# A gated low-rank FFN behind a per-sample matrix: the block products taken of x itself, the per-sample matrix applied to their rows

## Chip, cores and metric

One Trainium2 chip, one NeuronCore of it. The metric is device time in microseconds, here the median of three runs. All data is fp32.

## What is computed

x is 64 samples of 64 rows and 1024 columns. Each sample picks one of 16 matrices W (64x64), which turns the 64 rows of the sample into 64 tokens. A token is a vector of 1024; there are 4096 tokens.

```
W = weights[condition]
y = einsum('bct,bcd->bdt', x, W)            # 4096 tokens of 1024
scores = y @ Wr.T                           # 64 experts
top_vals, top_idx = top_k(scores, 16)
G = zeros.at[rows, top_idx].set(softmax(top_vals))
h = einsum('nd,krd->nkr', y, A)             # 64 experts x rank 16 = 1024
out = einsum('nkr,kdr->nd', h * G[:, :, None], B)
result = x + 2.0 * out
```

So there are two products with 1024x1024 matrices, "h" (with A) and "o" (with B), a gate between them, a small product with W ahead, and the routing.

## The kernel before

Tokens are worked on in 8 groups of 512 (4 tiles of 128). For each group, in this order:

- `condition` (L165 to L179): 4 tiles of x, each multiplied by its two W's in 64x64 matmuls (four at once, one per quadrant of the array) into PSUM tiles `yp`. ScalarE copies these into `y`, which holds y transposed. W's are fetched by an indirect DMA on GpSimd (`gather`, L129), with indices that VectorE computes from `cond`.
- `scores_t`, `scores` (L187 to L207): y times Wr in 128x256 matmuls (`st`), turned by a small matmul (`sp`); `route`/`route_top` on VectorE find the top 16, with exponentials on ScalarE; `gates` (L305) turns the gates into `gg`.
- the product h = A y, as a Strassen-Winograd scheme: y and A are split into 2x2 blocks of 512x512 (256 tokens), and 7 block products p1 to p7 replace 8. Sums of y's blocks are made on VectorE (`y_sums`).
- the results are added up in `hb` and multiplied by `gg` (L679, or L429 in the first two groups).
- the product o = hb B in the same scheme, added to x (loaded again, tiles `o`), and stored.

**One level and two levels.** Group 0 does both products on one level, group 1 does h on one level: `experts_in` (L398), `experts_out` (L460), which run `seven` (L353), in matmuls of 256 columns (h) or 512 (o). All else is on two levels: each of the 7 block products (a "parent", L569) is itself split into 7 leaf products. `run` (L622) issues one parent: leaf products p1, p2, then p3 of the parent before, p6, p4 of the parent before, then what is hooked in at "mid", then `prepare` of the next parent, then p7, p5, then what is hooked in at "end". `prepare` makes four sums t1 to t4 of the token operand on VectorE (256 elements a partition each); p5, p6, p7, p3 read them. Partial results meet in PSUM banks x, y, w and are combined by three copies and an add chain on ScalarE and VectorE. `done` adds parents up.

In an h parent of before A's leaf is the stationary operand and the tokens move, in matmuls of 128 columns, 4 per leaf product. In an o parent the tokens are stationary and B's leaf moves, 256 columns, 2 per leaf product.

**Leaves.** The 49 leaves of B and 49 of A are made once (VectorE differences, `leaf_steps`, L508) and stored to DRAM. All of B's, and three of each seven of A's, are then fetched for each parent on SP's queue into a ring of 11 buffers, in the order of their use (`order_of_use`, L545; `fetch`, L552, which runs after each use of a leaf). Four leaves of each block of A stay in SBUF. B's leaves are made during group 0's o product through a pool of three buffers (`bsum`), A's during group 1's h product, after the first fetches and residual loads of group 1 are already on the queue.

The order of work is written by hand; each engine runs its instructions in program order, SP too. A DMA on SP's queue also waits for the one that used its completion semaphore before, so some eight are in flight.

Of the kernel before, what the change touches and what calls it, by code (L numbers as in the profile page):

```python
# [15 lines left out]
P = 128  # L16
# [4 lines left out]
TPG = 4  # L21


@with_exitstack
def kernel(
    ctx: ExitStack,
    tc: tile.TileContext,
    x: bass.AP,
    cond: bass.AP,
# [5 lines left out]
):  # L35

# [17 lines left out]
    CH = HT // P  # L54
    HN = TPG * P // 2
    assert 2 * C == P and C == D and KR == T and HT == BANK and TOPK == 16
# [5 lines left out]
    xp = ctx.enter_context(tc.tile_pool(name="xp", bufs=4))  # L62
    small = ctx.enter_context(tc.tile_pool(name="small", bufs=2))
    acc = ctx.enter_context(tc.tile_pool(name="acc", bufs=7, space=PSUM))
# [3 lines left out]
    one_level = ctx.enter_context(ExitStack())  # L68
    tmp = one_level.enter_context(tc.tile_pool(name="tmp", bufs=1, side="right"))
    first_group = ctx.enter_context(ExitStack())  # L70
    bpool = first_group.enter_context(tc.tile_pool(name="bpool", bufs=1, side="right"))
    op = first_group.enter_context(tc.tile_pool(name="op", bufs=5, side="right"))
# [9 lines left out]
    cond_b = const.tile([P, B], I32)  # L82
    nc.sync.dma_start(cond_b, cond.to_broadcast([P, B]))
    xs = {}

    def load_x(i: int):
        xs[i] = xp.tile([P, T], F32, tag="x", name=f"x_{i}")
        nc.sync.dma_start(xs[i], x[ts(i, P), :])

    def load_block(name, src, r, c, pool=apool):  # L90
        t = pool.tile([P, CH, BANK], F32, name=name)
        nc.sync.dma_start(t, src[ts(r, HT), ts(c, BANK)].rearrange("(c p) k -> p c k", p=P))
        return t

    load_x(0)
    load_x(1)
    a11 = load_block("a11", a_t, 0, 0)
    load_x(2)  # L100
    load_x(3)
# [36 lines left out]
    wr_sb = const.tile([P, 2 * CH, K], F32)  # L138
    nc.sync.dma_start(wr_sb, wr_t.rearrange("(c p) k -> p c k", p=P))

    behind = const.tile([1, 1], F32)
    nc.sync.dma_start(behind, ws[0][0:1, 0, 0:1])
    a21 = load_block("a21", a_t, 0, 1)
    a22 = load_block("a22", a_t, 1, 1)
    a12 = load_block("a12", a_t, 1, 0)
    b12 = load_block("b12", b_t, 0, 1, bpool)
    b22 = load_block("b22", b_t, 1, 1, bpool)
    b11 = load_block("b11", b_t, 0, 0, bpool)
    b21 = load_block("b21", b_t, 1, 0, bpool)

    y, hb, yt = {}, {}, []
    for i in range(2):
        yt.append(blocks.tile([P, 2 * CH, HN], F32, name=f"y{i}"))
        for j in range(2):
            y[j, i] = yt[i][:, ts(j, CH), :]
            hb[i, j] = blocks.tile([P, CH, HN], F32, name=f"hb{i}{j}")
    gg = blocks.tile([P, TPG * P], F32, name="gg")

    def condition(g: int, i: int):

        xt = xs.pop(g * TPG + i)  # L165
        yp = [acc.tile([P, 2 * CH, D], F32, tag="acc", name=f"yp_{g}_{i}_{j}") for j in range(2)]
        for c in range(2 * CH):
            for j in range(2):
                r = slice(j * C, (j + 1) * C)
                for e in range(2):  # L170
                    nc.tensor.matmul(  # L171
                        yp[j][e * D : (e + 1) * D, c, :],
                        lhsT=xt[r, ds(c * P + e * D, D)],
                        rhs=ws[g][r, i, :],
                        start=True,
                        stop=True,
                    )
        for j in range(2):
            nc.scalar.copy(yt[i // 2][:, :, ds(i % 2 * P + j * D, D)], yp[j])  # L179

    def scores_t(g: int):

        st = ps_s.tile([P, 2, HN], F32, tag="s", name=f"st_{g}")
        for h in range(2):
            for c in range(2 * CH):
                e = slice((c % 2) * K, (c % 2 + 1) * K)
                nc.tensor.matmul(  # L187
                    st[e, h, :],
                    lhsT=wr_sb[:, c, :],
                    rhs=y[c // CH, h][:, c % CH, :],  # L190
                    start=(h == 0 and c < 2),
                    stop=(c >= 2 * CH - 2),
                    skip_group_check=True,
                )
        st_sb = small.tile([P, 2 * HN], F32, tag="st_sb", name=f"st_sb_{g}", bufs=1)
        nc.scalar.copy(st_sb, st.rearrange("p h n -> p (h n)"))
        return st_sb

    def scores(g: int, st_sb):

        sp = ps_s.tile([P, TPG, K], F32, tag="s", name=f"sp_{g}")
        for i in range(TPG):
            nc.tensor.matmul(
                sp[:, i, :], lhsT=st_sb[:, ts(i, P)], rhs=two_i, start=True, stop=True
            )
        scs = small.tile([P, TPG, K], F32, tag="sc", name=f"sc_{g}", bufs=1)
        nc.vector.tensor_copy(scs, sp)  # L207
        return scs

    def route(g: int, scs, i: int):  # L210

        sc = scs[:, i, :]
        top = small.tile([P, 16], F32, tag="top", name=f"top_{g}_{i}")
        left = small.tile([P, K], F32, tag="left", name=f"left_{g}_{i}", bufs=1)
        left2 = small.tile([P, K], F32, tag="left2", name=f"left2_{g}_{i}", bufs=1)
        nc.vector.max(top[:, 0:8], sc)
        neg = small.tile([P, 1], F32, tag="neg", name=f"neg_{g}_{i}")
        nc.vector.tensor_scalar(neg, top[:, 0:1], -1.0, None, ALU.mult)
        e = small.tile([P, K], F32, tag="e", name=f"e_{g}_{i}")
        nc.scalar.activation(e, sc, AF.Exp, bias=neg, scale=1.0)  # L220
        nc.vector.match_replace(
            out=left, in_to_replace=top[:, 0:8], in_values=sc, imm_value=TAKEN
        )
        nc.vector.max(top[:, 8:16], left)
        nc.vector.match_replace(
            out=left2, in_to_replace=top[:, 8:16], in_values=left, imm_value=TAKEN
        )
        gu = small.tile([P, K], F32, tag="gu", name=f"gu_{g}_{i}", bufs=1)
        total = small.tile([P, 1], F32, tag="total", name=f"total_{g}_{i}")
        nc.vector.scalar_tensor_tensor(  # L230
            gu, left2, TAKEN, e, ALU.is_le, ALU.mult, accum_out=total
        )
        inv = small.tile([P, 1], F32, tag="inv", name=f"inv_{g}_{i}")
        nc.vector.reciprocal(inv, total)
        g2 = small.tile([P, 2, K], F32, tag=f"g2_{i}", name=f"g2_{g}_{i}", bufs=1)
        nc.vector.tensor_scalar(
            g2,
            gu.unsqueeze(1).to_broadcast([P, 2, K]),
            inv,
            SCALING,  # L240
            ALU.mult,
            ALU.mult,
        )
        return g2

    def route_top(g: int, scs):

        top = rt.tile([P, TPG, 16], F32, tag="tops", name=f"tops_{g}")
        neg = rt.tile([P, TPG], F32, tag="negs", name=f"negs_{g}")
        e = rt.tile([P, TPG, K], F32, tag="es", name=f"es_{g}")  # L250
        total = rt.tile([P, TPG], F32, tag="totals", name=f"totals_{g}")
        inv = rt.tile([P, TPG], F32, tag="invs", name=f"invs_{g}")
        for i in range(TPG):
            nc.vector.max(top[:, i, 0:8], scs[:, i, :])
        nc.vector.tensor_scalar(neg, top[:, :, 0], -1.0, None, ALU.mult)

        def exps(*tiles):
            for i in tiles:
                nc.scalar.activation(
                    e[:, i, :], scs[:, i, :], AF.Exp, bias=neg[:, i : i + 1], scale=1.0  # L260
                )

        def rest(i):
# [3 lines left out]
                out=left, in_to_replace=top[:, i, 0:8], in_values=scs[:, i, :], imm_value=TAKEN  # L267
# [18 lines left out]
        def scaled():  # L286
            g2s = []
            for i in range(TPG):
                g2 = small.tile([P, 2, K], F32, tag=f"g2_{i}", name=f"g2_{g}_{i}", bufs=1)
                nc.scalar.activation(  # L290
                    g2,
                    e[:, i, :].unsqueeze(1).to_broadcast([P, 2, K]),
                    AF.Copy,
                    scale=inv[:, i : i + 1],
                )
                g2s.append(g2)
            return g2s

        return exps, rest, scaled

    def gates(g: int, g2s):

        gp = ps_s.tile([P, TPG, P], F32, tag="s", name=f"gp_{g}")
        for i in range(TPG):
            nc.tensor.transpose(gp[:, i, :], g2s[i].rearrange("p a k -> p (a k)"), ident)  # L305
        nc.scalar.copy(gg.rearrange("p (i n) -> p i n", n=P), gp)

    t3_pool = [extra]

    def y_sums():  # L310

        operands = {"p1": y[0, 0], "p2": y[1, 0], "p3": y[1, 1], "p5": y[0, 1]}

        def step1():
# [14 lines left out]

        return operands, step1, step2, step3  # L330

    def h_sums():

# [721 lines left out]
```

## Time and profile before

| | us |
|---|---|
| median of 3 runs | 815.12 (814.99 to 816.27) |
| the profiled execution | 819.59 |
| its span, first to last instruction | 817.3 |
| VectorE busy | 611.0 |
| TensorE weight loads busy (beside the matmuls) | 692.1 |
| granted TensorE clock, mean | 0.997 |

The page of a profile lists busy time by engine: PE are matmuls, PEld weight loads, DVE VectorE, ACT ScalarE, POOL GpSimd, SP the queue on which most DMAs are issued. Stretches give busy time in a window of the span; the chain of waits gives what the last instruction hung on; timelines give instructions by start. A program's fp32 matmul shows as two instructions. Lengths of matmuls overlap, so that costs are read from the distance between starts. Most of the data moved is leaves, in lines of the page's sixth part:

```profile
lo_p_p<-o_p_p SPq DMA_DIRECT2D x343, 256.0 KB
lh_p_p<-h_p_p SPq DMA_DIRECT2D x126, 256.0 KB
```

202.48 MB are moved in all, 248 GB/s over the span.

### The profile page before, as it was taken

To read this page: it belongs to the slowest core of one execution; us is meant where nothing else is said; L and a number is where in the kernel's file an instruction comes from. 1 tells how busy PE (TensorE), PEld (TensorE's weight loads), DVE (VectorE), ACT (ScalarE), POOL (GpSimd) and SP (SyncE) were. 2 spreads that over 40 slices of the span, in tenths; PEclk is the share of its full clock that TensorE was granted. 3 is DMA by queue.
4 is the path that set the end of the run, shared out by engine and by line. 5 is a ranking of instruction groups with operands and counts; after the bars stand their busy time and mean duration, and the time that the engine had idled before them with its cause. 6 is when DMAs were issued, how large, how long until landed. Compare 5 with 4: busy or idle time off the path is not lost.

```text
span 817.3 us, 17350 instructions
## 1 busy us (share of the span) xinstructions
PE 792.3 (97%) x6684; PEld 692.1 (85%) x6684; DVE 611.0 (75%) x1275; ACT 198.6 (24%) x507; POOL 35.3 (4%) x39
## 2 busy tenths in 40 slices
PE   2999998999999999999999999999999999999996
PEld 2888544888899988999889998899889998899985
DVE  0768447678897778968698686986879777896886
ACT  1110200102222232222323232332322323222221
POOL 4200200000200010000200002000000000000000
PEclk9999999999999999999999999999999999999999
DMA  8901568865889667894688856797678956787695
GB/s 286 386 32 40 187 232 295 315 234 189 270 268 391 196 208 232 300 386 146 193 285 324 307 168 216 262 364 245 192 221 287 387 181 201 243 304 253 181 301 200
DMA packets 108961, 202.48 MB, mean 248 GB/s; under 512 B 12114, under 2 KB 17490, under 8 KB 108882
## 3 DMA queue, kind: packets, MB, share of 16 engines
q1 hardware_dynamic: 107858, 200.35, 72.6%
q0 software_dynamic: 1024, 1.05, 0.5%
q8 instruction: 53, 0.87, 0.4%
q14 instruction: 26, 0.21, 0.1%
HBM read 166.23 MB, written 35.13 MB: 246 GB/s over the span
## 4 chain that ended last, share of the span: by engine, by line
PE 93%; DVE 2%; DMA 2%; issue 0%; ACT 0%; SPq 0%; DVEq 0%; ACTq 0%
PE o_p_x L596 21%; PE h_p_x L596 18%; PE o_p_w L596 11%; PE h_p_w L596 9%; PE o_p_y L596 5%; PE yp L171 5%; PE h_p_y L596 5%; PE st L187 4%; PE h_x L406 3%; PE h_z L406 3%; PE h_w L406 3%; PE o_z L465 2%; PE o_w L465 1%; PE o_x L465 1%; PE h_y L406 1%; DMA o_p_p<-os_p_p 1%
## 5 line engine op out<-in xcount | busy, mean ns | idle before, releaser
L596 PE MATMUL o_p_x<-lo_p_p,l_t 128*128 128x256 f32 x588 | 144.2, 379 | 0.5 <-ACT l_b L634 0.5
L596 PEld LDWEIGHTS o_p_x<-lo_p_p,l_t 128*128 128x128 f32 x588 | 110.7, 190 | 15.4 <-ACT l_b L634 0.9
L76 DVE TENSOR_TENSOR o<-o,m_o_p 128x1024 f32<-128x1024 f32 x56 | 68.2, 1219 | 0.8
L179 ACT COPY y<-yp 128x512 f32<-128x512 f32 x64 | 34.3, 590 | 90.5 <-PE yp L171 90.5
L171 PEld LDWEIGHTS yp<-w_st,x 64*64 64x64 f32 x2048 | 35.1, 140 | 24.3 <-DMA w_st<-in_cw_dram,idx 12.1
L76 DVE TENSOR_TENSOR m_h_p<-h_p_w,l_a 128x256 f32<-128x256 f32 x42 | 17.8, 423 | 50.5 <-PE h_p_w L596 50.5
L129 POOL DMA_INDIRECT w_st<-in_cw_dram,idx x32 | 34.5, 1078 | 463.7 <-PE yp L171 451.5
L171 PE MATMUL yp<-w_st,x 64*64 64x64 f32 x2048 | 39.8, 227 | 13.9 <-DMA w_st<-in_cw_dram,idx 12.1
L596 PE MATMUL o_p_w<-lo_p_p,l_t 128*128 128x256 f32 x196 | 52.5, 390 | 0.0
L596 PE MATMUL h_p_x<-l_t,lh_p_p 128*128 128x128 f32 x336 | 44.4, 275 | 0.0
L596 PE MATMUL h_p_w<-l_t,lh_p_p 128*128 128x128 f32 x336 | 44.4, 275 | 0.0
L596 PEld LDWEIGHTS h_p_x<-l_t,lh_p_p 128*128 128x128 f32 x336 | 41.4, 192 | 0.3
L596 PEld LDWEIGHTS h_p_w<-l_t,lh_p_p 128*128 128x128 f32 x336 | 41.3, 192 | 0.3
L596 PEld LDWEIGHTS o_p_w<-lo_p_p,l_t 128*128 128x128 f32 x196 | 35.2, 190 | 6.9 <-issue 2.3
L634 ACT COPY l_b<-o_p_x 128x256 f32<-128x256 f32 x49 | 18.3, 373 | 90.7 <-PE o_p_x L596 90.7
L76 DVE TENSOR_TENSOR m_o_p<-o_p_w,l_a 128x256 f32<-128x256 f32 x49 | 20.5, 419 | 24.8 <-PE o_p_w L596 18.3
L76 DVE TENSOR_TENSOR m_o_p<-o_p_w,l_b 128x256 f32<-128x256 f32 x49 | 20.6, 421 | 24.6 <-ACT l_b L634 24.6
L634 ACT COPY l_b<-h_p_x 128x256 f32<-128x256 f32 x42 | 15.6, 373 | 90.8 <-PE h_p_x L596 90.8
L641 ACT COPY m_o_p<-o_p_x 128x256 f32<-128x256 f32 x49 | 18.3, 373 | 64.2 <-PE o_p_x L596 64.2
L406 PE MATMUL h_x<-y,a 128*128 128x256 f32 x128 | 30.4, 394 | 1.1 <-ACT y L179 1.1
L679 DVE TENSOR_TENSOR hb<-hb,gg 128x1024 f32<-128x1024 f32 x24 | 29.4, 1225 | 0.8
L406 PEld LDWEIGHTS h_x<-y,a 128*128 128x128 f32 x128 | 25.1, 198 | 5.6 <-ACT y L179 1.2
(163 smaller groups left out, 1596.5 us busy)
## 6 DMA issues: line engine op xcount, KB each, us to landing
lo_p_p<-o_p_p SPq DMA_DIRECT2D x343, 256.0 KB
lh_p_p<-h_p_p SPq DMA_DIRECT2D x126, 256.0 KB
x<-in_x_dram SPq DMA_DIRECT2D x32, 512.0 KB
o<-in_x_dram SPq DMA_DIRECT2D x28, 512.0 KB
out_dram<-o SPq DMA_DIRECT2D x28, 512.0 KB
o_p_p<-os_p_p SPq DMA_DIRECT2D x28, 256.0 KB
h_p_p<-hs_p_p SPq DMA_DIRECT2D x21, 256.0 KB
a<-in_a_t_dram SPq DMA_DIRECT2D x4, 1024.0 KB
```

The costliest lines, as they stand in the source:

```text
L76: nc.vector.tensor_tensor(o, a, b, ALU.add)
L129: nc.gpsimd.indirect_dma_start(out=w_st[:, i, :], out_offset=None, in_=cw, in_offset=bass.IndirectOffsetOnAxis(ap=idx[:, n : n + 1], axis=0),)
L171: nc.tensor.matmul(yp[j][e * D : (e + 1) * D, c, :], lhsT=xt[r, ds(c * P + e * D, D)], rhs=ws[g][r, i, :], start=True, stop=True,)
L179: nc.scalar.copy(yt[i // 2][:, :, ds(i % 2 * P + j * D, D)], yp[j])
L187: nc.tensor.matmul(st[e, h, :], lhsT=wr_sb[:, c, :], rhs=y[c // CH, h][:, c % CH, :], start=(h == 0 and c < 2), stop=(c >= 2 * CH - 2), sk ...
L406: nc.tensor.matmul(bank[:, ts(s, HN)], lhsT=left[p][:, c, ts(2 * q + s, P)], rhs=right[p][:, c, :], start=first and s == 0 and c == 0, sto ...
L465: nc.tensor.matmul(bank, lhsT=left[p][:, c, ts(m, P)], rhs=right[p][:, c, :], start=first and c == 0, stop=c == CH - 1, skip_group_check=True,
L596: nc.tensor.matmul(bank if kind == "o" else bank[:, ts(s, P)], lhsT=v[:, c, :] if kind == "o" else w[:, c, ts(s, P)], rhs=w[:, c, :] if ki ...
L634: nc.scalar.copy(par["val"][n], par["bank"]["x"])
L641: nc.scalar.copy(pr["q"][0][1], pr["shaped"](pr["bank"]["x"]))
L679: nc.vector.tensor_tensor(hb[i, j], hb[i, j], gg[:, ts(j, HN)].unsqueeze(1).to_broadcast([P, CH, HN]), ALU.mult,)
```

## The change

- The host also hands over x transposed and cut in blocks (`x_t`). The h product is taken of x's rows, not of the tokens: Z = A x per row, in the same scheme with the rows as the stationary operand and A's blocks moving. `gated` then multiplies Z's rows by W, again in 64x64 matmuls (`zp`), and the gate multiplication by `gg` reads these from PSUM and writes `hb`. `condition` and its ScalarE copies go.
- Scores are taken of x's rows too: `scores_t` and `turn` as before, and then `scores`, 8 more 64x64 matmuls with W (`sw`). ScalarE copies both results.
- There is one chain of parents, each on one or two levels. h and o parents have the same form: 256-column leaf products of two matmuls, or, on one level, two halves of four 512-column matmuls each, copied by ScalarE. Group 0 is on one level, and the first four h parents of group 1; the last three are on two levels.
- The sums of A and B are chosen such that both schemes have the form of o. p1, p2, p3 and p5 of A's leaves stay in SBUF. Of three B blocks (p1, p2, p3) the three raw leaves are fetched from B itself and not stored.
- The ring has 14 buffers. In group 1 the first 14 fetches and the residual loads come between A's leaves, in the order p7, p5, p3, fetches, residual loads, p1, p2, p4, p6.
- x_t of the next group is loaded at the end of the first o parent; x was loaded at the first h parent. The scores of the next group are still taken in the o parents; routing of tiles 2 and 3 falls in the first h parent.
- The first load is x_t's block 00 and A's block 11, each in two halves that alternate, and `cond` is loaded on ScalarE's queue.

The core of the diff:

```diff
+    def scores(st):
...
+        for i in range(TPG):
+            for j in range(2):
+                r = slice(j * C, (j + 1) * C)
+                nc.tensor.matmul(
+                    sw[r, i, :], lhsT=ws[g][r, i, :], rhs=st["zr"][r, i, :], start=True, stop=True
+                )
...
+    def gated(st, i, j):
...
+        for c in range(CH):
+            for s in range(2):
+                for b in range(2):
+                    r = slice(b * C, (b + 1) * C)
+                    for e in range(2):
+                        nc.tensor.matmul(
+                            zp[b][e * D : (e + 1) * D, c, s, :],
+                            lhsT=z[r, s, ds(c * P + e * D, D)],
+                            rhs=ws[g][r, 2 * i + s, :],
...
+        for b in range(2):
+            nc.vector.tensor_tensor(
+                tokens(hb[j, i])[:, :, :, b, :], zp[b], g_ij[:, :, :, b, :], ALU.mult
+            )
...
+            for c in range(2):
+                nc.tensor.matmul(
+                    bank,
+                    lhsT=v[:, c, :],
+                    rhs=w[:, c, :],
...
+    load_x(0, 0, 0, 2, (load_a11(0), load_a11(1)))
+    load_x(0, 1, 0)
+    a21 = load_block("a21", a_t, 1, 0, apool)
...
+        lv = {0: (1,) * 7, 1: (1, 1, 1, 1, 2, 2, 2)}.get(st["g"], (2,) * 7)
...
+        if g:
+            at(h + 0, "mid", sums, st, "x_sums", "s3")
...
+            at(h + 0, "mid", rest, st, 2, 3)
...
+        at(h + 2, "mid", load_res, st)
+        if g == 1:
...
+            at(h + 0, "mid", a_leaf, "p7")
+            at(h + 0, "end", a_leaf, "p5")
+            at(h + 1, "mid", a_leaf, "p3")
+            at(h + 1, "end", first_fetches)
+            at(h + 2, "mid", a_leaf, "p1")
+            at(h + 3, "mid", a_leaf, "p2")
+            at(h + 4, "end", a_leaf, "p4")
+            at(h + 5, "end", a_leaf, "p6")
+        if nxt:
...
+            for i, j in ((0, 0), (1, 0), (0, 1), (1, 1)):
+                at(o, "end", load_x, g + 1, i, j)
...
+            at(o + 2, "mid", scores_t, nxt)
```

Here `h + n` and `o + n` are the n-th parent of a group's h and o product, "mid" and "end" the places in `run`.

## The prediction

> **What bounds the kernel now.** I read the page first, then busy time by stretches, then the start of the chain of waits, then the timeline around places where TensorE slows down. The page's first part says which engine counts:
>
> ```profile
> span 817.3 us, 17350 instructions
> PE 792.3 (97%) x6684; PEld 692.1 (85%) x6684; DVE 611.0 (75%) x1275; ACT 198.6 (24%) x507; POOL 35.3 (4%) x39
> ```
>
> TensorE is busy 97%. Busy time by stretches (span of the stretch, then PE, PEld, DVE, ACT, POOL busy with counts, granted clock, DMA share, GB/s):
>
> ```profile
> 402.30:498.60 96.30, 96.30 (x890) 88.33 (x890) 75.94 (x164) 28.36 (x74) 4.28 (x4) 1.00 0.78 259
> 150.00:155.00 5.00, 5.00 (x26) 4.38 (x26) 3.55 (x16) 0.35 (x1) 0.00 (x0) 1.00 1.01 376
> 155.00:160.00 5.00, 5.00 (x26) 4.41 (x25) 2.46 (x4) 0.59 (x1) 0.00 (x0) 1.00 1.05 393
> ```
>
> One steady group of 512 tokens takes 96.3 us and TensorE never rests in it; VectorE has 20 us spare. The other two lines are a burst of loads: the DMA engines give about 385 GB/s when asked. The chain in its first 26 us (start, us, what) and TensorE's timeline (start, us, line, operation):
>
> ```profile
> 0.74 4.43 DMA cond_b<-in_cond_dram
> 6.07 5.94 DMA w_st<-in_cw_dram,idx
> ...
> 20.16 5.16 PE h_x L406 x16
> 25.31 2.02 PE yp L171 x128
> ```
>
> ```profile
> 25.24 2.10 PE L171 MATMUL yp<-w_st,x 64*64 64x64 f32 x128
> 128.67 5.40 PE L465 MATMUL o_z<-b,s 128*128 128x512 f32 x8 [2.16 <-DVE o_b L76]
> 133.90 3.60 PE L465 MATMUL o_w<-bt,hb 128*128 128x512 f32 x8
> 312.14 1.03 PE L596 MATMUL o_p_y<-lo_p_p,s 128*128 128x256 f32 x4
> 313.00 1.89 PE L596 MATMUL o_p_x<-lo_p_p,l_t 128*128 128x256 f32 x8
> 343.43 1.06 PE L596 MATMUL h_p_y<-y,a 128*128 128x128 f32 x8
> 344.32 1.06 PE L596 MATMUL h_p_x<-y,lh_p_p 128*128 128x128 f32 x8
> ```
>
> Lengths overlap, so I cost by distance of starts: a leaf product (two matmuls of 256 columns, or four of 128; each is two instructions) takes 313.00 - 312.14 = 0.86 us in the out product (0.863 over a run of them) and 344.32 - 343.43 = 0.89 (0.893) in the first product. A block product on one level takes 3.43 us per half in 512-column matmuls, 3.454 in 256-column ones.
>
> **The start.** Before, TensorE waits 12.05 us for cond, index and gather; at 25.24 it has done only 2.02 + 3.45 = 5.5 us of full-speed work, so it behaves as if started at 19.8. After, the first product reads x_00 and a11, loaded in halves: 0.25 + 0.5 MB. By stretches the DMAs before had moved 0.83 MB by 6 us; with an estimated 1 us to land, TensorE starts at 7.0. It starts at the low clock: the 5.16 row against 3.45 says 1.7, I take 2. Effective start 9.0: **10.8 saved**. Bounds: data at 6 (11.8) and at 10 (7.8). The later blocks (3 MB by 12 us, 6.3 MB by 20) come before their products, since each product takes 6.9 us. Gathering is now needed only for the scores, past 30 us.
>
> **Stalls of the first group.** At 46.67 a product of 3.45 ends at 50.1 and the next starts at 50.99, after a sum of A: 0.9. At 126.3 the product before the 128.67 row is through: 2.3 idle, plus 5.40 - 3.43 = 2.0 of low clock, because VectorE waited for leaf stores. **5.2 saved**: in the new order the one-level products need only ScalarE's copies of 0.6 us.
>
> **First product.** Groups 2 to 7 go from 49 leaf products at 0.893 to 49 at 0.863: 1.47 each, 8.8. Group 1 had 14 halves at 3.454 = 48.4 and gets 8 at 3.43 plus 21 leaves at 0.863 = 45.6: 2.8. Group 0: 0.3. **11.9 saved.** Here a rule would give less. The Trainium skill (TensorE: Matmul & The Clock Gate, Back-to-back issue gap) gives an isolated warm gap of N/2.4 + 2.5 ns. Taken twice per fp32 instruction it is 111.7 ns for 128 columns, which is the row (0.893/8), but 218.3 for 256, where the row is 215.8. By the rule a group saves 1.0, not 1.47, and the sum loses 2.9. The rows decide.
>
> **W's products move, they don't go.** 128 products of 64x64 per group stay (four runs of about 1.09, same shapes): 0. Two PSUM evictions per run go from ScalarE (0.59 each) into VectorE's gate, which now reads PSUM: 8 of 128x512 at 0.69 (the nearest row, a gate of a PSUM tile in the first groups) = 5.5 for 4 gates of 1.22 = 4.9. VectorE stays at about 76 of 96 us; on average it is cover enough. New are 8 matmuls of W on the scores' rows. No row shows two quadrants at work; four give 0.016 us per instruction, none would give 0.056: 16 instructions are 0.25 to 0.9. I take 0.5 and 0.1 for the switch: **4.8 lost** in 8 groups (2.8 to 8).
>
> **The end.** Before, VectorE does two adds of 1.24 just ahead of the last one. After, one: **1.1 saved**. The last store is the same.
>
> **Waits in a steady group.** VectorE's queue has tight places. At the first parent of a group it now does, ahead of the operands of the third, one x sum (1.2), two tiles' routing (1.05 each by the timeline) and reciprocals (0.4), where before it did one tile. Those operands are first needed 1.73 + 2.59 = 4.3 us after that place. Writing out the queue with 0.34 per 256-element operation (0.46 if dependent) and 1.15 per 1024 (1.25), from the scores on, operand t2 of the second parent comes 0.8 late. The gates are the other place: VectorE waits there for W's products, behind it queue the next parent's operands, and for those TensorE waits; three come in a row, and I find 0.5 to 1 to spare. So 0.8 in each of groups 2 to 7: **4.8 lost** (0 to 12). Next in line behind such a wait is only TensorE itself.
>
> **The jam in group 1.** This is the biggest unknown. VectorE makes A's leaves in group 1's first product, 4 operations of 0.69 for each of seven blocks, while it still makes B's last leaves. Time from the fifth out parent of group 0: VectorE is through with B's leaves at 22.4 without waiting for stores, about 26.5 with (three buffers, as at 126 us before). Then come x sum, routing, leaves of p7, p5, p3, ending near 41. After those SP gets 14 fetches (0.26 MB), then the 4 residual loads (0.52 MB), and only then the stores of the next leaves (p1). A's leaves have three buffers: the leaves of p2 can't be written before p1's stores land. At 385 GB/s the 6.0 MB take 15.7 us, with 2 us of latency (estimate): 58.7. Behind that wait VectorE has 2.8 of leaves and 0.9 until t2 of the first two-level parent: 62.4. TensorE wants t2 at 52.0. That is 10.4 of idling. And the clock: the skill's same page (The HAM clock gate) says it falls after an idle window of about 3.4 us; the 128.67 row lost 2.0 after 2.3 us of idling. By either rule this gap pays, so 2.0 more; VectorE's work in the next parents (6.5 to 7.7 against 6.05) costs another 1. **13.4 lost** (0 if VectorE is some 10 us earlier, 24 if stores go as slowly as at 116 to 130).
>
> **Other moves.** x_t is loaded at the first out parent (2 MB, contiguous) instead of in the next first product; it has 11.4 us until the scores and needs 2/0.385 + 2 = 7. It is moved onto the stretch with the most fetches (1.8 MB per 6 us, 297 GB/s); the ring of 14 holds two parents, 12 us, more than the 5 us that it delays them. 0, up to 6 lost. Three B blocks are fetched raw in 1 KB rows, 9 of 49 fetches: 0, up to 2 lost. Copying scores to ScalarE (24% busy): 0.
>
> **Sum.** Saved 10.8 + 5.2 + 11.9 + 1.1 = 29.0; lost 4.8 + 4.8 + 13.4 = 23.0; net 6.0. The profiled execution took 819.59 (span 817.3, 2.3 around it), so its successor takes 813.6; the median is 4.5 below the profiled one: 815.12 - 6.0 = **809.1**.
>
> **Rivals.** *The cover holds* (0.18): no jam, no late t2. For it: VectorE has 20 us spare per group, and the leaf stage before shows no idle TensorE. Against: there the fetches were issued ahead of all of A's leaves, here between them. 809.1 - 18.2 = 790.9.
> *The jam decides, slower* (0.22): one mechanism, SP's queue with stores behind fetches. At 113 to 131 ten leaf steps took 18 us, 1.8 each; if the last 13 B steps go so, 23.4 in place of 9 plus the 4 of waiting that I allowed, everything behind is 10.5 later: 819.6. It turns the sign once group 1 waits over 13.4 + 6.0 = 19.4 us. Against: fewer raw blocks are stored, and no loads lie among those stores.
> *It doesn't shorten a group* (0.12): the late operand costs 1.8 instead of 0.8 in six groups, so that a steady group stays longer than 96.3, and the gain at the start is eaten: 815.1, no change.
> My forecast has 0.48. The likeliest cases of both signs lie apart; the forecast's own range is 803 to 815.
>
> **Numbers.** Within 0.2% (1.6 us) is about what a measurement can't tell from no change. Faster: 0.46 of the forecast, 0.18, and 0.02 of the third rival; same: 0.02 and 0.10; slower: 0.22. The range 790 to 821 reaches to the first rival's time and a little beyond the slower one's, and leaves out about half of the first and a third of the slower one.
>
> **What would show it.** Start: TensorE's first matmul at 6 to 8 us. First product: 0.863 between starts of leaf products. Steady group: 95.5 to 97 between two score products, with a gap of about 0.8 at the second parent's third operand, released by VectorE. Jam: a gap of some 10 us ahead of group 1's first two-level parent, VectorE waiting for a store of A's p1. No such gap, and I am wrong towards 791; gaps in several places of group 1, and towards 820. A first matmul after 10 us or steady groups over 98 would break the sum too.

## The result, and the profile after

| | before | after |
|---|---|---|
| median, first comparison | 815.48 (814.99 to 816.27, 4 runs) | 822.97 (822.09 to 824.54, 4 runs) |
| median, second comparison, in a later set of runs | 820.16 (818.4 to 821.7, 17 runs) | 823.75 (821.64 to 824.27, 5 runs) |
| the profiled execution, and its span | 819.59, 817.3 | 823.33, 821.3 |
| mean granted TensorE clock | 0.997 | 0.991 |

The change made the kernel slower: the ratio is 1.0093 [1.0075, 1.0111] in the first comparison and 1.0045 [1.0031, 1.0058] in the second. So the loss is under 1% and clear of the noise in both. The changed kernel takes nearly the same time in both. It is the kernel before that varies: four runs at 815 to 816, and all 66 of the later sets at 818.4 to 823.3. The profiled execution of before (819.59) belongs to the second level, and so does a second profile of it that was taken later (821.08); steady groups are 96.36 long in both.

The page's first lines after:

```profile
span 821.3 us, 14798 instructions
PE 788.6 (96%) x5448; PEld 617.6 (75%) x5448; DVE 614.0 (75%) x1279; ACT 194.4 (24%) x509; POOL 32.8 (4%) x39
```

TensorE is busy for 3.7 us less and rests for longer: 25.0 us idle before, 32.7 after. So the question is where it rests. Its timeline after, at the start and in group 1 (start, us, line, operation, and in brackets the idle time just before and who ended it):

```profile
8.49 16.61 PE L459 MATMUL h_p<-a,x 128*128 128x512 f32 x32 [8.49 <-DMA a<-in_a_t_dram]
25.04 3.67 PE L180 MATMUL st<-x,wr_sb 128*64 128x256 f32 x32
...
150.67 1.16 PE L303 MATMUL zp<-w_st,m_h_p 64*64 64x64 f32 x64 [2.08 <-DVE m_h_p L81]
...
156.16 1.03 PE L493 MATMUL h_p_y<-at,x 128*128 128x256 f32 x4
169.08 2.05 PE L493 MATMUL h_p_x<-lh_p_p,l_t 128*128 128x256 f32 x4 [11.90 <-issue]
...
174.29 1.03 PE L493 MATMUL h_p_x<-a,sum_p 128*128 128x256 f32 x4
```

From 25.04 to 148.6 TensorE never rests: group 0's stalls are gone. Ahead of 150.67 it waits 2.1 us for a sum on VectorE. At 156.16 + 0.86 it wants operand t2 of the first two-level parent and gets it at 169.08, 12.1 us late. The next three leaf products then take 5.2 us (169.08 to 174.29) where 2.6 is normal. Who holds the operand is seen on VectorE's timeline, and why on SP's (columns as above; on SP the length is that of issuing):

```profile
165.31 0.69 DVE L84 TENSOR_TENSOR hs_p_p<-a 128x512 f32<-128x512 f32 x1 [12.09 <-DMA h_p_p<-hs_p_p]
```

```profile
145.89 3.79 SPq L425 DMA_DIRECT2D lh_p_p<-h_p_p  x8
149.72 1.13 SPq L425 DMA_DIRECT2D lo_p_p<-in_b_t_dram  x2
151.53 0.34 SPq L425 DMA_DIRECT2D lo_p_p<-o_p_p  x1
152.20 0.34 SPq L425 DMA_DIRECT2D lh_p_p<-h_p_p  x1
152.81 0.97 SPq L425 DMA_DIRECT2D lo_p_p<-o_p_p  x2
154.15 2.77 SPq L610 DMA_DIRECT2D o<-in_x_dram  x4
157.28 11.25 SPq L389 DMA_DIRECT2D h_p_p<-hs_p_p  x6
```

VectorE wants a buffer for a leaf of A's p2 and waits 12.09 us for a store of p1. That store stands behind 14 fetches and 4 residual loads: the first of p1's stores is issued at 157.28, 11.4 us after the first fetch, and lands 8.0 us later. (The 11.25 us of the last line are not all SP's own time: three of its six stores are p2's, and for these SP waits until VectorE has made the leaves.) By stretches (PE, PEld, DVE, ACT, POOL busy, granted clock, DMA share, GB/s) the queue's bytes run at full rate while all engines stand still, and when TensorE starts again, it does so at half clock:

```profile
158.00:164.00 6.00, 0.00 (x0) 0.00 (x0) 0.00 (x0) 0.00 (x0) 0.00 (x0) 0.72 1.05 389
164.00:170.00 6.00, 0.92 (x2) 0.84 (x3) 4.55 (x10) 0.00 (x0) 0.00 (x0) 0.50 0.61 233
```

In a steady group two things are new on TensorE's timeline, W on the scores (first line) and a gap at the second parent of the first product:

```profile
320.28 0.68 PE L211 MATMUL sw<-zr,w_st 64*64 64x64 f32 x16
...
342.58 1.03 PE L493 MATMUL h_p_x<-a,l_t 128*128 128x256 f32 x4
344.29 1.10 PE L493 MATMUL h_p_x<-lh_p_p,l_t 128*128 128x256 f32 x4 [0.68 <-ACT m_h_p L528]
...
346.21 1.03 PE L493 MATMUL h_p_w<-lh_p_p,l_t 128*128 128x256 f32 x4
```

344.29 - 342.58 is 1.71, 0.85 over a leaf product's 0.86. The two products behind the gap take 0.1 longer each: 346.21 - 342.58 is 3.63 for three products that take 2.59 elsewhere, so the late operand costs 1.04. The record names ScalarE, whose copy ends at 344.01; VectorE's t2 ends later, at 344.19, and the routing experiment shows that it is the one that counts. Between two score products' starts a group takes 96.75 (303.50 to 400.25); before, the same milestones lay 96.36 apart.

### The profile page after: what moved, and what is told of

The parts are those of the page before. It is cut to its first block, busy times and chain, and to the rows that moved or that the text cites. A ratio compares the mean times of both kernels' runs of the same rounds, so it can differ in the third digit from the quotient of the medians.

```text
span 821.3 us, 14798 instructions
## 1 busy us (share of the span) xinstructions
PE 788.6 (96%) x5448; PEld 617.6 (75%) x5448; DVE 614.0 (75%) x1279; ACT 194.4 (24%) x509; POOL 32.8 (4%) x39
## 4 chain that ended last, share of the span: by engine, by line
PE 91%; DVE 3%; DMA 2%; issue 2%; ACT 0%; SPq 0%; DVEq 0%; ACTq 0%
PE o_p_x L493 21%; PE h_p_x L493 19%; PE o_p_w L493 11%; PE h_p_w L493 10%; PE h_p L459 7%; PE o_p_y L493 5%; PE h_p_y L493 5%; PE o_p L459 4%; PE zp L303 4%; PE st L180 4%; DMA o_p_p<-os_p_p 1%; DMA a<-in_a_t_dram 1%; DVE hs_p_p L84 1%; PE sp L197 1%; PE sw L211 1%
## 5 line engine op out<-in xcount | busy, mean ns | idle before, releaser
L81 DVE TENSOR_TENSOR m_h_p<-m_h_p,m_h_p 128x1024 f32<-128x1024 f32 x56 | 67.5, 1218 | 0.3
L493 PE MATMUL h_p_x<-lh_p_p,l_t 128*128 128x256 f32 x180 | 47.7, 388 | 16.0 <-issue 11.9
L316 DVE TENSOR_TENSOR hb<-zp,gg 128x512 f32<-128x512 f32 x64 | 41.2, 686 | 21.2 <-PE zp L303 21.2
L493 PE MATMUL h_p_x<-a,l_t 128*128 128x256 f32 x208 | 53.4, 379 | 0.0
L493 PEld LDWEIGHTS h_p_x<-lh_p_p,l_t 128*128 128x128 f32 x180 | 34.1, 193 | 23.0 <-issue 12.3
L493 PE MATMUL h_p_w<-lh_p_p,l_t 128*128 128x256 f32 x180 | 48.5, 392 | 0.0
L493 PEld LDWEIGHTS h_p_x<-a,l_t 128*128 128x128 f32 x208 | 39.5, 190 | 5.4
L493 PE MATMUL h_p_x<-at,l_t 128*128 128x256 f32 x152 | 39.8, 385 | 0.0
L303 PE MATMUL zp<-w_st,m_h_p 64*64 64x64 f32 x2048 | 37.2, 221 | 2.1 <-DVE m_h_p L81 2.1
L493 PEld LDWEIGHTS h_p_w<-lh_p_p,l_t 128*128 128x128 f32 x180 | 33.2, 193 | 4.8
```

Source lines behind the costliest of these rows:

```text
L81: nc.vector.tensor_tensor(o, a, b, ALU.add)
L303: nc.tensor.matmul(zp[b][e * D : (e + 1) * D, c, s, :], lhsT=z[r, s, ds(c * P + e * D, D)], rhs=ws[g][r, 2 * i + s, :], start=True, stop=True,
L316: nc.vector.tensor_tensor(tokens(hb[j, i])[:, :, :, b, :], zp[b], g_ij[:, :, :, b, :], ALU.mult)
L493: nc.tensor.matmul(bank, lhsT=v[:, c, :], rhs=w[:, c, :], start=first and c == 0, stop=c == 1, skip_group_check=True,)
```

## The experiments

The runs were made in four sets, and the kernel before ran beside each of them: its medians there were 820.56, 820.16, 820.29 and 820.22. So these sets can be compared with one another to about 0.5 us, and "less" in what follows means less than the changed kernel's 823.75.

| run | median us | ratio to before | group 1 | steady group |
|---|---|---|---|---|
| changed kernel again | 823.75 | 1.0045 [1.0031, 1.0058] | 118.6 | 96.75 |
| six buffers for A's leaves | 812.18 | 0.989 [0.9874, 0.9906] | 108.7 | 96.75 |
| fetches behind the leaves | 815.88 | 0.994 [0.992, 0.9961] | 112.8 | 96.75 |
| routing spread | 818.44 | 0.9973 [0.9959, 0.9987] | 119.3 | 96.08 |
| no W on the scores | 815.61 | 0.9948 [0.9934, 0.9961] | 116.4 | 95.94 |
| warm start | 820.26 | 1.0002 [0.9993, 1.001] | 117.9 | 96.75 |
| leaves late | 811.87 | 0.99 [0.9885, 0.9915] | 102.3 | 96.75 |
| residual loads later | 817.28 | 0.9965 [0.9953, 0.9977] | 114.6 | 96.75 |
| first loads in quarters | 819.61 | 0.9992 [0.9984, 1.0] | 119.2 | 96.75 |
| losses taken away together | 803.96 | 0.9799 [0.9786, 0.9812] | 102.3 | 96.68 |
| the best version | 799.02 | 0.974 [0.9727, 0.9754] | 102.3 | 96.07 |

Group 1 is the distance between the starts of the score products (`st`) of groups 1 and 2 in the run's profile, the steady group that of groups 3 and 4.

**The jam: buffers, place in the queue, bytes, place on VectorE.** Four runs ask what makes group 1 long.

```diff
-        for n, b in (("bp", RING), ("lp", 2), ("lt", 2), ("al", 3)):
+        for n, b in (("bp", RING), ("lp", 2), ("lt", 2), ("al", 6)):
```

> A's leaves get six buffers in place of three; nothing else changes. My theory (the stores of p1's leaves stand behind 14 fetches and 4 loads on SP's queue, and VectorE can't write p2's leaves before they land): VectorE's wait of 12.1 us ahead of p2's leaves goes, with it TensorE's gap of 11.9 us and the 2.6 us of low clock behind it; the 2.25 us ahead of the first W products stay. 14.5 us less than the changed kernel: about 808.5. Rival (VectorE is late by its own work in group 1, the wait for the store only shows where it stands): less than 4 us gained, 819 or more.

The gap is gone, and 11.6 us with it, 2.9 less than the theory wanted. VectorE no longer needs p1's stores when it makes p2's leaves. 3.1 us of new gaps (1.88 and 1.26) appear one and two parents later: VectorE now waits for the same stores at the leaves of p4.

```profile
165.29 0.69 DVE L84 TENSOR_TENSOR hs_p_p<-at 128x512 f32<-128x512 f32 x1 [4.08 <-DMA h_p_p<-hs_p_p]
```

```diff
+        at(h + (3 if g == 1 else 2), "mid" if g != 1 else "end", load_res, st)
...
-            at(h + 1, "end", first_fetches)
...
             at(h + 3, "mid", a_leaf, "p2")
+            at(h + 3, "mid", first_fetches)
```

> Three buffers as in the changed kernel, but the first 14 fetches and the residual loads of group 1 are issued behind p1's and p2's leaves. My theory: the same gap goes, 12 to 14.5 us gained, 808.5 to 811, perhaps with 1 to 2 us of waiting for the first fetched leaf, which now is issued some 4 us before its use. Rival (VectorE's own work): 819 or more.

The same three buffers, but no stores of p1 and p2 behind fetches: the gap of 12 is gone here too, 7.9 us less, and not 12 to 14.5. What comes instead is that the fetches are now late themselves:

```profile
158.74 1.50 PE L493 MATMUL h_p_x<-lh_p_p,l_t 128*128 128x256 f32 x4 [2.24 <-DMA lh_p_p<-h_p_p]
```

TensorE waits 2.24 us for a fetched leaf, and at 179.75 another 2.25 for VectorE; behind each gap it loses 1.8 more by the low clock. Either cure works alone, so it takes both, few buffers and a long queue, to make the jam.

```diff
-        at(h + 2, "mid", load_res, st)
+        at(h + (3 if g == 1 else 2), "end" if g == 1 else "mid", load_res, st)
```

> Only the four residual loads of group 1 (2.1 MB) are taken out from between the fetches and the leaf stores; they are issued behind the stores of p2. Theory (VectorE waits for p1's stores, which stand behind 14 fetches and 4 residual loads on SP's queue, so the wait is as long as their bytes take): at 385 GB/s 5.4 us go from the gap of 12, 6 to 7 stay, and with them the low clock afterwards; 5 to 6 us less than the changed kernel. Rival 1 (the number of buffers is all, not the queue's bytes): the gap stays at 11 to 12 and the time the same. Rival 2 (the residual loads were the whole of it): gap under 2, 13 us less.

This varies the amount: 2.1 MB fewer stand ahead of the stores, and the gap shrinks by 5.0:

```profile
163.49 2.05 PE L493 MATMUL h_p_x<-lh_p_p,l_t 128*128 128x256 f32 x4 [6.86 <-issue]
```

6.86 in place of 11.90, as the theory said (6 to 7), with the low clock behind it kept; 6.5 us less. At the 389 GB/s of the stretch above, 2.1 MB take 5.4 us: the wait is about as long as the bytes take that stand ahead.

```diff
-            at(h + 2, "mid", a_leaf, "p1")
-            at(h + 3, "mid", a_leaf, "p2")
-            at(h + 4, "end", a_leaf, "p4")
-            at(h + 5, "end", a_leaf, "p6")
+            at(o + 0, "end", a_leaf, "p1")
+            at(o + 2, "end", a_leaf, "p2")
+            at(o + 3, "end", a_leaf, "p4")
+            at(o + 5, "end", a_leaf, "p6")
```

> The leaves of A's blocks p1, p2, p4 and p6, which only group 2 reads, are made in group 1's out product (one block behind each of its parents 0, 2, 3 and 5) instead of in its first product; buffers and fetches stay. Theory (group 1 loses 16.9 us to VectorE's leaves and to their stores behind the fetches): no gap ahead of group 1's first two-level parent, no late sum ahead of its first gated block, group 1 about 101 to 104 us between its score products' starts in place of 119: 15 to 17 us less than the changed kernel, if the out product has room for 11 us of VectorE. Rival 1 (VectorE's whole load in group 1 is the limit, its place is of no matter): 4 to 9 us less, with gaps in the out product. Rival 2 (the burst of 14 fetches is itself late for its users): 7 to 10 less, with a gap that waits for a fetched leaf.

Group 1 fell to 102.3, with no gap at all in its first product: the late sum ahead of `zp` (150.67 above, 2.1 us) was VectorE's leaves too. But the time fell by 11.9 and not by 15 to 17. Group 2 took 102.8 instead of 96.75, and TensorE's timeline says where:

```profile
191.86 1.08 PE L180 MATMUL st<-x,wr_sb 128*64 128x256 f32 x8 [0.42 <-DMA x<-in_x_t_dram]
```

```profile
227.75 1.83 PE L493 MATMUL h_p_x<-lh_p_p,l_t 128*128 128x256 f32 x4 [3.00 <-issue]
229.37 1.91 PE L493 MATMUL o_p_w<-lo_p_p,sum_p 128*128 128x256 f32 x4
```

The load of x_t now stands behind the stores of p1's leaves on SP's queue (issued from 181.99, the load from 184.53), and the scores wait for it. On VectorE the leaves of p6 (221.23 to 224.0) run just ahead of the routing and the operands of group 2's first two-level parent (3.00 idle, then half clock). So neither the theory nor its rivals were wholly right: the place of the leaves decides, but not every place has room.

**The late operand.**

```diff
-            at(h + 0, "mid", rest, st, 2, 3)
+            at(h + 0, "mid", rest, st, 2)
+            at(h + 1, "mid", rest, st, 3)
```

> Routing of the fourth tile goes from the first to the second first-product parent of a group, as in the kernel before. Theory (VectorE's queue at the first parent makes operand t2 of the second late): the gap of 0.85 to 0.95 us in each of groups 2 to 7 goes, a steady group falls from 96.75 to 95.8 us, 5.7 us in all: 817.3. Rival (the gap is set by ScalarE's copy, which the record names as its releaser, or moves to the third parent, whose operands now queue behind the routing): 821 or more.

The gap at the second parent goes, and a steady group takes 96.08, 0.67 less and not 0.95: a gap of 0.27 comes up one parent later, at 349.32, since the routing is now ahead of the next operands. It costs 0.37 with the slower product behind it, and 0.67 + 0.37 are the 1.04 from above. Over six groups 0.67 is 4.0 us; the medians of the two runs differ by 5.3. It also shows that the releaser named in the record (ScalarE) wasn't it: only VectorE's order was altered, and now the product starts at 343.01, ahead of ScalarE's copy (343.21).

The edit moves tile 3 in group 1 too. There the gates are made later, and TensorE waits for them:

```profile
142.95 1.35 PE L287 MATMUL gp<-ident,g 128*128 128x128 f32 x4 [1.57 <-ACT g L275]
144.10 5.18 PE L459 MATMUL h_p<-at,x 128*128 128x512 f32 x8
```

The gap and the low clock behind it cost 4.0 us, and as the jam's gap is 1.8 shorter and the wait at `zp` is gone, group 1 takes 119.3 as before.

**W on the scores.** This kernel leaves out W on the scores' rows: the routing then works on other numbers, with the same instructions.

```diff
-        for i in range(TPG):
-            for j in range(2):
-                r = slice(j * C, (j + 1) * C)
-                nc.tensor.matmul(
-                    sw[r, i, :], lhsT=ws[g][r, i, :], rhs=st["zr"][r, i, :], start=True, stop=True
-                )
-        nc.scalar.copy(scs, sw)
+        nc.scalar.copy(scs, st["zr"])
```

> The scores are taken of x's rows alone: W on the scores' rows (8 matmuls of 64x64 per group) is left out, so the routing is of other numbers, while all later work is the same in kind and number. Theory (these matmuls are on TensorE's path, 0.82 us a group as read from the distances of starts): 6.6 us less than the changed kernel. The prediction's size (0.6 a group) would give 4.8. Rival (their time is slack that another wait takes over, such as the late operand): 0 to 2.

8.1 us less. A steady group is 0.81 shorter and group 0 too; that is 6.5 in 8 groups. Group 1 gained 1.3 more than that, because its two gaps are 1.1 shorter in this profile. No other wait took the place over.

**The start.**

```diff
+    zero = const.tile([P, P], F32)
+    nc.vector.memset(zero, 0.0)
+    idle = acc.tile([P, P], F32, tag="acc", name="idle")
+    for _ in range(22):
+        nc.tensor.matmul(idle, lhsT=zero, rhs=zero, start=True, stop=True)
```

> 22 matmuls of 128 columns on a tile of zeros run before the first data is there, into a PSUM tile that nobody reads. Theory (the first 5.5 us of products run at half speed because TensorE comes out of rest): the first 32 products take 13.8 us instead of 16.6, 2.5 to 3 us less in all; the first real product starts at 8.5 as before. Rival (the slow first products wait for data, that is for the loads of x and A): 0. If the 22 matmuls end after 8.5, less than that is gained.

```profile
1.06 7.18 PE L134 MATMUL idle<-zero 128*128 128x128 f32 x44 [1.06 <-DVE zero L131]
8.39 13.97 PE L466 MATMUL h_p<-a,x 128*128 128x512 f32 x32 [0.15 <-issue]
```

The first 32 instructions take 13.97 in place of 15.5 to 16.8 (nine profiles of kernels without the zeros). They start when they did before and run through, so it was the clock that held them and not the data. 3.5 us less; by the profiles 1.6 to 2.8 of it is the start, and the rest lies in group 1 (117.9), where nothing was altered.

```diff
-    load_x(0, 0, 0, 2, (load_a11(0), load_a11(1)))
+    load_x(0, 0, 0, 4, [load_a11(k) for k in range(4)])
```

(`load_a11` loads a quarter then.)

> The first loads (block 00 of x_t and A's block 11) come in quarters instead of halves, so that the first product needs 0.13 + 0.25 MB. Theory (the first product came at 8.5 instead of 7.0 because its 0.75 MB shared the queue with the loads behind them): first matmul at 6.5 to 7.5 us, 1 to 2 us less than the changed kernel. Rival (what holds it is the time until the first transfers land at all, and the order of loads is of no matter): first matmul at 8.2 to 8.6, 0. The low clock at the start is the same in both.

```profile
5.48 16.35 PE L459 MATMUL h_p<-a,x 128*128 128x512 f32 x32 [5.48 <-DMA a<-in_a_t_dram]
```

First matmul at 5.48, 3.0 earlier and a microsecond better than the theory; 4.1 us less. So the first product's start hung on how many bytes it asks for, half of them here.

**All of it together.** Six buffers; the leaves of p1 and p2 behind the h parents 4 and 5 and those of p4 and p6 behind the o parents 1 and 3; the 22 zeros; and routing, from group 2 on, pulled ahead:

```diff
-            at(h + 0, "mid", rest, st, 2, 3)
+            at(h + 0, "mid", rest, st, *((2, 3) if g == 1 else (3,)))
...
-            at(o + 6, "mid", rest, nxt, 0, 1)
+            if g:
+                at(o + 5, "end", rest, nxt, 0)
+            at(o + 6, "mid", rest, nxt, *((1, 2) if g else (0, 1)))
```

> The changed kernel with each loss that has been named so far taken away: TensorE is warmed by 22 matmuls on zeros; A's leaves have six buffers, those of p1 and p2 are made after the fetches, behind group 1's h parents 4 and 5, those of p4 and p6 behind its o parents 1 and 3; from group 2 on, routing of tile 0 is done one place earlier (end of o parent 5), of tiles 1 and 2 in o parent 6, and only tile 3 in the first h parent. Theory (these are separate terms that add up: 3.4 of the start, 15 to 17 of group 1, 5.7 of the late operand, with W on the scores left as it is): 24 to 26 less than the changed kernel, ratio to the kernel before 0.973 to 0.977; group 1 101 to 104 us, steady groups 95.8. Rival (VectorE has no room for leaves and earlier routing, so that the waits come back elsewhere): 13 to 18 less, with steady groups of 96.2 and over or group 2 over 98.

19.8 less, not 24 to 26. Group 1 (102.3) and the start (first 32 instructions 13.97) are as expected. The steady group isn't: 96.68. Pulling the routing ahead only moved the late operand to the parent before, where TensorE now waits 0.47 by the record and 0.63 by distance of starts. This part of the theory fell: moving a tile's routing to a later parent, as above, gains, and moving it to an earlier place gained next to nothing.

The last run puts tile 3 into the second parent instead (from group 2 on), and loads in quarters with 11 zeros in place of 22:

> As the kernel with the losses taken away together, with two things altered: the routing of tile 3 moves to the second h parent (from group 2 on) and tiles 0 to 2 go back to their places, and the first loads come in quarters, with 11 matmuls on zeros instead of 22. Theory: the late operand gives 0.67 a group back in groups 2 to 7 (4.0), which the earlier routing did not; the quarters bring 2.5 to 3: 796 to 798, steady groups 96.0 to 96.1, first real product at 5.5 to 6. Rival (the steady group cannot be shortened once the leaves of A lie in the out product, or the zeros still run when the first data is there): 800 to 804.

Its page and the start of TensorE's timeline:

```profile
span 796.9 us, 14849 instructions
...
PE 788.3 (99%) x5470; PEld 620.2 (78%) x5470; DVE 613.6 (77%) x1280; ACT 194.9 (24%) x509; POOL 32.8 (4%) x39
```

```profile
1.06 5.06 PE L134 MATMUL idle<-zero 128*128 128x128 f32 x22 [1.06 <-DVE zero L131]
5.92 14.91 PE L466 MATMUL h_p<-a,x 128*128 128x512 f32 x32
```

799.02 at a ratio of 0.974 [0.9727, 0.9754] beats both kernels; it lies 1 above the range that was expected. The steady groups are (96.07) and the first product is (5.92) where they should be; the first 32 instructions take 14.91, 0.9 more than behind 22 zeros. The first two of them lose 0.6 below full speed, so 11 zeros weren't enough; the rest is a wait of 0.3 at 13.72, whose cause the profile doesn't name. TensorE is busy 99%, with the same 788 us as in the changed kernel. Against the kernel before it gains 21 us, with all of the change still in it. That isn't the worth of the change: the zeros and smaller first loads were not tried on the kernel before.

## Why the prediction was wrong, by its own steps

The forecast of 809.1 missed 822.97 by 13.9. Terms in us; measured values are from the profile after, by distances of starts:

| step | predicted | measured |
|---|---|---|
| start | saved 10.8 | saved 8.5 |
| stalls of group 0 | saved 5.2 | saved 5.4 |
| first product | saved 11.9 | saved 11.9 |
| end | saved 1.1 | saved 0.7 |
| W on the scores | lost 4.8 | lost 6.6 |
| late operand, six groups | lost 4.8 | lost 6.2 |
| jam in group 1 | lost 13.4 | lost 16.9 |
| sum | net 6.0 saved | net 3.2 lost |
| from the profiled execution to the median | 4.5 below | 0.4 below |

The mechanisms were the right ones, in their places. The three losses were taken 6.7 too small in all and two savings 2.7 too large; with 0.2 the other way at the stalls that is 9.2 us, enough to turn the sign. The profiled executions differ by 3.7 and not by 3.2, so 0.5 isn't accounted for. The last row brings the other 4.1.

- **"The start ... 10.8 saved".** Failed in size. Data came at 8.49 and not at 7.0: the prediction took the rate at which all loads together moved before, and 1 us to land that no row shows, but the first 0.75 MB had other loads in flight beside them. The low clock took 2.8 in this profile instead of 2 (1.7 to 3.0 in the nine kernels that start cold). 25.04 less 13.74 of full-speed work is an effective start of 11.3, against 19.8.
- **"Stalls of the first group", "First product".** Held: no idle time from 25 to 148, and 0.8635 between leaf products. That the stalls' sum came out is in part luck. The product said to start at 46.67 starts at 46.77, so that its stall is 0.8, and the low clock behind 128.67 took 1.8 (5.40 is a length, 3.43 a distance); a stall of 0.6 ahead of 46.77 wasn't counted. The row decided rightly against the rule weighed there (the Trainium skill, TensorE: Matmul & The Clock Gate, Back-to-back issue gap), which would have given 1.0 a group.
- **"16 instructions are 0.25 to 0.9. I take 0.5".** The matmuls of W on two quadrants take 0.61, and with the switches to and from them a group pays 0.82 (0.81 by the run without them). Two quadrants in turn are 0.038 an instruction, halfway between four (0.016) and the bound of none (0.056).
- **"0.8 in each of groups 2 to 7".** The queue written out by hand was right: the gap is 0.85. The 0.2 that the two products behind a gap take longer stood in no term, so a group loses 1.04. With these 1.04, 0.82 for W and 1.45 saved by shorter leaf products (49 at 0.893 against 49 at 0.8635), a steady group comes out 0.4 longer, as measured (96.75 against 96.36).
- **"The jam ... 13.4 lost".** The prediction put the landing of p1's stores 17.7 after the fetches begin (6.0 MB at 385 GB/s, and 2); it was 19.4 (145.89 to 165.31). The first 13 us gave only 318 GB/s, which fits a later landing. So the gap is 12.1 instead of 10.4. The low clock took 2.6 instead of 2.0. And a gap of 2.2 ahead of the first gated block, where VectorE is late by A's leaves (it is gone where these are made later), stood in no term; in its place "another 1" of late operands was put, which didn't show. 12.1 + 2.6 + 2.2 = 16.9, inside the bounds given, and well short of the 19.4 at which the prediction let the sign turn: that point held every other term fixed.
- **"The median is 4.5 below the profiled one".** The worst single step, at 4.1. The distance belonged to the kernel before on that occasion, not to profiling: after, the profiled run lies within 0.4 of its median, and later runs of before have their median at 820.2 to 820.6, near where its two profiles lay (819.59 and 821.08). Without it the forecast would have been 813.6. Why four runs of before were 5 us faster stays open: none of them left a trace.

Of the rivals, "the jam decides" came close in time (819.6) but by another sum, and that is luck: it wanted B's leaves 10.5 later than the 26.5 allowed, and they were done 28.2 after the fifth out parent's start (102.54 to 130.7), 1.7 later. The range (790 to 821) ended 2 us too low, since it reached to the rivals' times but gave no error to the small terms and to the step from the profile to the median, and nearly all of these misses pointed one way.

## What to carry to other kernels

A store that frees a buffer and stands behind a burst of loads on the same queue waited here for the burst's bytes (12.1 us on VectorE behind 5.8 MB): count them, and either give the pool as many buffers as are written meanwhile, or put the burst behind the stores. When work is taken off the busiest engine, look at whether the engine that feeds it has its spare time where it is now needed: here VectorE had 20 us spare a group, and still was late in the places that the change gave it; with its leaves and routing moved, more buffers, and a start warmed up and fed in smaller loads, the slower kernel became the faster. A sum of many terms needs an error for each, and a distance between a profile and a median is no property of the kernel: here it was 4.5 before and 0.4 after.

## What the runs showed of the hardware

- TensorE starts at half speed and stays there for over 4 us of work. The matmuls on zeros in the warm start show it by stretches (PE busy with instructions, PEld, granted clock, DMA share, GB/s):

```profile
4.00:5.00 1.00, 1.00 (x6) 1.00 (x6) 1.00 0.87 295
5.00:6.00 1.00, 1.00 (x10) 1.00 (x9) 1.00 0.90 272
6.00:7.00 1.00, 1.00 (x12) 1.00 (x11) 1.00 1.00 340
```

  Six instructions a microsecond become twelve a little after 5 us, with work since 1.06. The granted clock reads 1.00 all the same. Behind rests in the middle of a run it does show the half: 0.50 behind the gap of group 1 after, and behind the 2.16 us of before. So at the start the rate has to be read from distances. In the best version half speed lasted until about 7.2.
- Rests of 1.6 to 2.5 us went both ways, and the idle window of about 3.4 us that the prediction weighed was not needed. 1.57 us with the routing spread cost 2.3 of low clock, 2.16 us ahead of the 128.67 row of before 1.8, and 2.25 with the fetches behind the leaves 1.8. 2.08 us at 150.67 after and 2.51 with six buffers cost none (the half behind them took 3.54 us, as behind `zp` elsewhere). 3.00 and 11.90 us cost 1.8 and 2.6. Why the same rest does one or the other stays open.
- The first product, asking for 0.38 MB, could start 5.48 us after the start of the span, on the same queue on which it started at 8.49 when it asked for 0.75 MB.
